# Reading x once in the mixing stage of a two-layer mixture-of-experts kernel: channel-major products, square transposes, permuted rank matrices

## The chip, the core and the metric

The kernel runs on one core of a Trainium2 chip. The metric is device time in microseconds (us), the median of three runs. A profile of one further execution goes with it: its own time, its span (from the first to the last instruction), and every instruction and transfer in it.

Engines, as the profile names them: PE is TensorE (matrix products), PEld its weight loads, DVE is VectorE, ACT is ScalarE, POOL is GpSimd, SP is SyncE, which here only issues transfers. A name with a q at the end (ACTq, SPq) is the engine's queue issuing a transfer.

## The reference, cut to what matters

The input x has 32 batches of 128 rows by 1024 channels, all float32. Two layers follow one another:

```python
# layer 0: each batch picks one of 200 matrices and mixes its rows with it; then a mixture of experts
h = einsum('bct,bcd->bdt', x, weights[cond])        # 32 x 128 tokens x 1024 channels
logits = h @ gate_w.T                               # 64 experts
w, sel = top_k(softmax(logits), 8); w /= w.sum()
# token order fixes the slot of a token at its expert; 256 slots each, later ones are dropped
x = x + scatter_add(w * (silu(inp @ wg) * (inp @ wu)) @ wd)
# layer 1: a linear map with a chosen low-rank part, then a second linear map with 8 gated low-rank parts
x = x + L1_ffn(L1_cond(x))
```

The change concerns the first line and the routing only: how h is made, scored and stored, and how the list of tokens of each expert is found.

## The kernel before, in words

The kernel has three stages. **Stage A** (lines 319 to 552) makes h, routes it and writes it to a buffer in device memory, `hbuf`; on the side it folds weight matrices for the last stage. **Stage B** (lines 658 to 719) is a loop over 64 experts: GpSimd gathers the tokens of an expert from `hbuf`, PE makes the products `pp` and `po`, and GpSimd adds the result to `ybuf`, a second buffer, which has to hold a copy of x by then. **Stage C** (lines 917 to 1021) is a loop over 16 pairs of batches with the products `pr_c`. Nearly every instruction outside the expert loop is recorded at line 206, since the helper `InOrder` issues it; so the tile names are what tells instructions apart. That helper also keeps the instructions of each engine in the order of the program.

Stage A goes in 8 groups of 4 batches. The steps that the change and the prediction touch:

- `loaded_turned(b)` (line 328) loads batch b of `x_t`, a copy of x that the host has turned so that channels lie on partitions: the tile `xTb`, 512 KB, 4 buffers.
- `loaded_batch(b)` (line 332) has GpSimd gather the mixing matrix of the batch, `w`, by row numbers, and SP load batch b of x with rows on partitions: the tile `x`, 512 KB, 6 buffers. So every batch of x is read in two layouts.
- `scored(g)` (line 344): 8 products per batch with a 128x128 block of `xTb` as weights and 64 columns of the gate matrix moving, into `pxg`; VectorE copies it to `xg`.
- `logits(g, xg)` (line 380): one product per batch of `w` with `xg` gives the 64 scores of each token, `plog`; VectorE finds the best 8, ScalarE takes the exponentials.
- `mixed(b)` (line 362): two products per batch, `w` as weights and 512 columns of x moving, into `ph`; ScalarE copies the one half, VectorE the other, to `h` (3 buffers), which ScalarE's queue writes to `hbuf`.
- `counted(g, mask, wt)` (line 410): products with the triangular matrix `tri` and with `ident` give each token's rank at each expert and its weight, turned (`prk`), which ScalarE copies and writes to `ranks` in device memory; a product with `ones` counts tokens per expert (`pcnt`), which VectorE adds up in `upto`.
- `carried(b)` (line 375): SP copies batch b of x to `ybuf`, from device memory to device memory. 24 batches are copied in the loop, the last 8 after it (line 493).
- `combined(n, d)` (line 429): the side work for stage C, 8 products of 388 columns, `pcw`. 9 such steps lie in the loop of groups, 9 after it.

A product of float32 operands is issued as two PE instructions; so 8 products are 16 instructions in the profile.

Behind the groups, `looked_up` (line 214) finds from `upto` in which batch and at which rank each slot of an expert lies; `fetched` (line 235) gathers those rows of `ranks` with GpSimd (`rkg`); `found` (line 253) turns ranks into token numbers on VectorE, and a small product `prow` spreads them over the four quarters of a token's row; `placed` (line 293) makes row numbers out of them, `slot_row`; `gathered` (line 299) fetches the quarters of the tokens from `hbuf`. Two and a half steps of `combined` stand on PE between the last `counted` and the first `prow`.

Of the kernel before, what the change touches and what calls it, by code (L numbers as in the profile page):

```python
# [8 lines left out]
F32 = mybir.dt.float32  # L9
# [42 lines left out]
def kernel(  # L52
# [6 lines left out]
    x_t: bass.AP,  # L59
    gate_w: bass.AP,  # L60

# [20 lines left out]

    hbuf = dram.tile([NT + P, H], F32, name="hbuf")
# [12 lines left out]
    tri = const.tile([P, P], F32, name="tri")  # L96
    nc.gpsimd.affine_select(
        tri, ones, pattern=[[1, P]], compare_op=ALU.is_ge, fill=0.0, base=0, channel_multiplier=-1
    )
# [30 lines left out]
    nc.vector.tensor_scalar(inquad, quad, -float(Q), pcol, ALU.mult, ALU.add)  # L130
    qmask = const.tile([P, NQ], F32, name="qmask")
# [121 lines left out]
    def found(some, lo, hi):  # L253
        u = some["u"] + lo
        n = (hi - lo) * NJ
        flat = some["batch"][:, lo:hi, :].rearrange("p e j -> p (e j)")
        rank = some["rank"][:, lo:hi, :].rearrange("p e j -> p (e j)")
        rk = some["rk"][:, lo * NJ : hi * NJ, :, :]
        hit = fs.tile([P, n, P], F32, name=f"hit_{u}", tag="hit")
        place = fs.tile([P, n], F32, name=f"place_{u}", tag="place")  # L260
        dve.tensor_tensor(
            hit, rk[:, :, 0, :], rank.unsqueeze(2).to_broadcast([P, n, P]), ALU.is_le
        )
        dve.tensor_reduce(place, hit, AX.X, ALU.add)
        dve.tensor_tensor(
            hit,
            iota_t.unsqueeze(1).to_broadcast([P, n, P]),
            place.unsqueeze(2).to_broadcast([P, n, P]),
            ALU.is_equal,
        )  # L270
        dve.tensor_tensor(hit, hit, rk[:, :, 1, :], ALU.mult)
        mine = slice(u * NJ, u * NJ + n)
        dve.tensor_reduce(slot_w[:, mine], hit, AX.X, ALU.add)
        empty = fs.tile([P, n], F32, name=f"empty_{u}", tag="empty")
        dve.tensor_scalar(empty, flat, float(NB), pcol, ALU.is_equal, ALU.mult)
        dve.tensor_tensor(place, place, empty, ALU.add)
        tok = fs.tile([P, n], F32, name=f"tok_{u}", tag="tok")
        dve.scalar_tensor_tensor(tok, flat, float(P), place, ALU.mult, ALU.add)
        byq = fs.tile([P, n, NQ], F32, name=f"byq_{u}", tag="byq")
        dve.tensor_tensor(  # L280
            byq,
            tok.unsqueeze(2).to_broadcast([P, n, NQ]),
            qmask.unsqueeze(1).to_broadcast([P, n, NQ]),
            ALU.mult,
        )
        dve.tensor_copy(slot_tok[:, mine], tok)
        prow = pf.tile([P, 512], F32, name=f"prow_{u}", tag="prow")[:, 0 : n * NQ]
        pe.matmul(
            prow, spread, byq.rearrange("p s q -> p (s q)"), start=True, stop=True
        )  # L290
        some["prow"] = (slice(u * NJ * NQ, (u * NJ + n) * NQ), prow)

    def placed(some):
        rows, prow = some["prow"]
        dve.tensor_scalar(slot_row[:, rows], prow, float(NQ), quad, ALU.mult, ALU.add)
# [23 lines left out]
    with (  # L319
# [6 lines left out]
        xs, xTs, ws = {}, {}, {}  # L326

        def loaded_turned(b):
            xTs[b] = a6.tile([P, HC, P], F32, name=f"xTb_{b}", tag="xTb", bufs=4)
            sync.dma_start(xTs[b].rearrange("p j c -> p (j c)"), x_t[b])  # L330

        def loaded_batch(b):
# [7 lines left out]
            xs[b] = a6.tile([P, H], F32, name=f"x_{b}", tag="x_t")  # L340
            sync.dma_start(xs[b], x[b])


        def scored(g):
            pxg = pa_sm.tile([P, GB, E], F32, name=f"pxg_{g}", tag="sm")
            for t in range(GB):
                xT_b = xTs.pop(g * GB + t)
                for j in range(HC):
                    pe.matmul(
                        pxg[:, t, :],  # L350
                        xT_b[:, j, :],
                        gw_sb[:, j, :],
                        start=(j == 0),
                        stop=(j == HC - 1),
                    )
            xg = a2.tile([P, GB, E], F32, name=f"xg_{g}", tag="xg")
            dve.tensor_copy(xg, pxg)
            for b in range((g + 1) * GB, min((g + 2) * GB, NB)):
                loaded_turned(b)
            return xg  # L360

        def mixed(b):
            rows = slice(b * P, (b + 1) * P)
            h_sb = a2.tile([P, H], F32, name=f"h_{b}", tag="h_sb", bufs=3)
            for n in range(2):
                cols = slice(n * 512, (n + 1) * 512)
                ph = pa_big.tile([P, 512], F32, name=f"ph_{b}_{n}", tag="big")
                pe.matmul(ph, ws[b], xs[b][:, cols], start=True, stop=True)
                if n == 0:
                    act.copy(h_sb[:, cols], ph)  # L370
                else:
                    dve.tensor_copy(h_sb[:, cols], ph)
            act.dma_start(hbuf[rows, :], h_sb)
# [4 lines left out]


        def logits(g, xg):  # L380
            plog = pa_sm.tile([P, GB, E], F32, name=f"plog_{g}", tag="sm")
            for t in range(GB):
                pe.matmul(plog[:, t, :], ws[g * GB + t], xg[:, t, :], start=True, stop=True)
            top = a2.tile([P, GB, K], F32, name=f"top_{g}", tag="top")
            left = a2.tile([P, GB, E], F32, name=f"left_{g}", tag="left")
            for t in range(GB):
                dve.max(top[:, t, :], plog[:, t, :])
                dve.match_replace(left[:, t, :], top[:, t, :], plog[:, t, :], LOW)
            nmax = a2.tile([P, GB], F32, name=f"nmax_{g}", tag="nmax")
            dve.tensor_scalar(nmax, top[:, :, 0], -1.0, None, ALU.mult)  # L390
            ex = a2.tile([P, GB, E], F32, name=f"ex_{g}", tag="ex")
            for t in range(GB):
                act.activation(ex[:, t, :], plog[:, t, :], AF.Exp, bias=nmax[:, t : t + 1])
            mask = a2.tile([P, GB, E], F32, name=f"mask_{g}", tag="mask")
            dve.tensor_scalar(mask, left, LOW, None, ALU.is_equal)
            return ex, mask

        def weights_of(g, ex, mask):
            wt = a2.tile([P, GB, E], F32, name=f"wt_{g}", tag="wt")
            dve.tensor_tensor(wt, ex, mask, ALU.mult)  # L400
# [5 lines left out]
            return wt  # L406
# [3 lines left out]
        def counted(g, mask, wt):  # L410
            rk_sb = a2.tile([E, GB, 2, P], F32, name=f"rk_{g}", tag="rk", bufs=1)
            for i in range(2):
                prk = pa_sm.tile([E, 2, 2, P], F32, name=f"prk_{g}_{i}", tag="sm")
                for t in range(2):
                    pe.matmul(prk[:, t, 0, :], mask[:, 2 * i + t, :], tri, start=True, stop=True)
                    pe.matmul(prk[:, t, 1, :], wt[:, 2 * i + t, :], ident, start=True, stop=True)
                act.copy(rk_sb[:, 2 * i : 2 * i + 2, :, :], prk)
            act.dma_start(ranks[:, g * GB : (g + 1) * GB, :, :], rk_sb)
            pcnt = pa_sm.tile([P, GB, E], F32, name=f"pcnt_{g}", tag="sm")
            pe.matmul(pcnt, ones, mask, start=True, stop=True)  # L420
            for t in range(GB):
# [3 lines left out]
                else:  # L425
                    dve.tensor_tensor(upto[:, :, b], upto[:, :, b - 1], pcnt[:, t, :], ALU.add)

# [14 lines left out]

        gw_sb = a1.tile([P, HC, E], F32, name="gw_sb")
        loaded_turned(0)
        sync.dma_start(gw_sb.rearrange("p j e -> p (j e)"), gate_w)
        for b in range(1, GB):
            loaded_turned(b)
        for b in range(6):
            loaded_batch(b)
# [7 lines left out]
        NG = NB // GB  # L457
        rest = [(0, d) for d in range(HC + 1)]
        xg = scored(0)
        hws = {0: head_block(0)}  # L460
        lefts = left_block("a", 0, "wd")
        for g in range(NG):
            ex, mask = logits(g, xg)
            for t in range(GB):
                b = g * GB + t
                mixed(b)
                if t == 1:
                    wt = weights_of(g, ex, mask)
                if b + 6 < NB:
                    loaded_batch(b + 6)  # L470
                if b >= 8:
                    carried(b - 8)
            if g == NG - 2:
# [6 lines left out]
            for _ in range((0, 1, 1, 1, 1, 1, 2, 2)[g]):  # L480
                for _ in combined(*rest.pop(0)):
                    pass
            if g + 1 < NG:
                xg = scored(g + 1)
                if g == 0:
                    lefts += left_block("a", 1, "wd")
                    lefts += left_block("a", 2, "wu")
                if g == 4:
                    hws[1] = head_block(1)
            counted(g, mask, wt)  # L490
# [606 lines left out]
```

## Time and profile before

| quantity | value |
|---|---|
| time, median of 3 runs (lowest, highest) | 2785.03 us (2782.26, 2787.5) |
| profiled execution, its own time | 2768.09 us |
| its span | 2766.4 us |
| PE busy in the span | 2729.5 us, 99% |
| DVE, ACT, POOL busy | 57%, 15%, 41% |
| bytes moved by transfers | 585.11 MB, mean 212 GB/s |
| last product of the last `counted` of stage A ends | 218.86 us |
| first product of the expert loop | 277.13 us |
| last expert product ends, stage C's own begin | about 2140 us |

Matrix products overlap one another in the record, and a product that waits for its weights counts as busy; so a busy share of 99% does not mean that PE is at its peak. What a product costs is read from the distance between starts in a row of equal ones. The chain of work that ended last names, at each step, what the step waited for; a product in it is on the path that sets the end. The granted clock (PEclk) says at what share of its full rate PE was allowed to run in a stretch.

### The profile page before, as it was taken

What the parts mean: (1) busy time and instruction counts of PE and PEld (TensorE: products, weight loads), DVE (VectorE), ACT (ScalarE), POOL (GpSimd) and SP (SyncE); (2) the same over time, 40 slices, a digit from 0 to 9 for tenths busy, and PEclk for the clock granted to TensorE, in tenths of its full rate; (3) what the DMA queues carried; (4) which work ended last, traced back from release to release, by engine and by line L of the source; (5) the groups of instructions that cost most, each with busy time, mean ns of one, the idle gap of its engine ahead of it and who ended that gap; (6) DMA issues with size and microseconds to landing.
All of it is one profiled execution on the core that took longest, in us unless ns stands there. A gap on an engine that the chain in (4) does not pass through costs nothing.

```text
span 2766.4 us, 23669 instructions
## 1 busy us (share of the span) xinstructions
PE 2729.5 (99%) x8580; PEld 1513.0 (55%) x8580; DVE 1581.5 (57%) x2521; ACT 408.6 (15%) x792; POOL 1123.1 (41%) x846
## 2 busy tenths in 40 slices
PE   8998999999999999999999999999999899999999
PEld 6765555555555555555555555555555555555554
DVE  2334667666676666766657667576563444444442
ACT  1220111111111111111111111111111000000000
POOL 2105365555655646556465564655451100000000
PEclk9999999999999999999999999999999999999999
DMA  9997777777878878777787777777775522222210
GB/s 349 381 376 263 238 255 227 248 262 225 251 241 243 255 225 252 256 234 248 235 249 254 229 247 253 241 244 238 237 248 153 137 74 62 62 61 65 60 43 38
DMA packets 131141, 585.11 MB, mean 212 GB/s; under 512 B 23312, under 2 KB 50000, under 8 KB 105168
## 3 DMA queue, kind: packets, MB, share of 16 engines
q1 hardware_dynamic: 71136, 405.18, 39.6%
q0 software_dynamic: 51200, 155.24, 24.3%
q10 hardware_dynamic: 8688, 23.17, 2.2%
q8 instruction: 68, 1.11, 0.2%
q14 instruction: 49, 0.40, 0.0%
HBM read 476.45 MB, written 123.83 MB: 217 GB/s over the span
## 4 chain that ended last, share of the span: by engine, by line
PE 96%; DMA 2%; DVE 1%; issue 0%; ACT 0%; SPq 0%; POOL 0%; ACTq 0%; DVEq 0%
PE pp L594 42%; PE po L693 23%; PE pr_c L206 17%; PE pcw L206 4%; PE px L206 2%; PE pxg L206 2%; PE ph L206 2%; PE pth L644 2%; DMA xTb<-in_x_t 1%; DMA hbuf<-h 1%; PE prk L206 1%; PE plog L206 0%; DMA rkg<-ranks,row 0%; PE pg L206 0%; PE pt L206 0%
## 5 line engine op out<-in xcount | busy, mean ns | idle before, releaser
L306 POOL DMA_INDIRECT xin<-hbuf,slot_row x512 | 722.6, 1411 | 159.2 <-issue 151.8
L693 PE MATMUL po<-wd,hTb 128*128 128x512 f32 x1536 | 680.3, 592 | 0.6 <-ACT hTb L646 0.6
L704 POOL DMA_INDIRECT ybuf<-o,slot_tok x128 | 205.3, 1604 | 666.1 <-ACT o L702 465.4
L693 PEld LDWEIGHTS po<-wd,hTb 128*128 128x128 f32 x1536 | 286.8, 190 | 323.7 <-issue 306.1
L594 PE MATMUL pp<-wg,xT 128*128 128x384 f32 x1024 | 351.6, 486 | 0.6 <-ACT G_sb L206 0.6
L594 PE MATMUL pp<-t,s 128*128 128x384 f32 x1024 | 341.9, 487 | 0.0
L594 PEld LDWEIGHTS pp<-t,s 128*128 128x128 f32 x1024 | 193.4, 190 | 141.9 <-issue 23.0
L206 DVE TENSOR_TENSOR u<-p,pp 128x384 f32<-128x384 f32 x64 | 35.4, 554 | 386.4 <-PE pp L594 386.4
L594 PEld LDWEIGHTS pp<-wg,xT 128*128 128x128 f32 x1024 | 189.6, 190 | 119.9 <-ACT G_sb L206 1.2
L702 ACT ACTIVATE o<-po,slot_w 128x512 f32<-128x512 f32 x256 | 175.9, 687 | 494.1 <-PE po L693 489.9
L206 POOL DMA_INDIRECT ab<-in_AT,adapter_rows x32 | 36.6, 1144 | 444.2 <-ACT pxw L206 438.9
L206 PE MATMUL pr_c<-BM,X 128*128 128x512 f32 x480 | 213.7, 592 | 0.0
L206 DVE STREAM_TRANSPOSE xT<-xin 128x1024 f32<-128x1024 f32 x128 | 156.1, 1235 | 67.6 <-DMA xin<-hbuf,slot_row 62.4
L594 PE MATMUL pp<-t,xT 128*128 128x384 f32 x512 | 175.6, 486 | 0.0
L594 PE MATMUL pp<-wu,xT 128*128 128x384 f32 x512 | 175.6, 486 | 0.0
L594 PE MATMUL pp<-wu,s 128*128 128x384 f32 x512 | 175.6, 486 | 0.0
L611 ACT ACTIVATE h<-gate 128x384 f32<-128x384 f32 x128 | 67.2, 525 | 699.6 <-DVE gate L206 699.6
L242 POOL DMA_INDIRECT rkg<-ranks,row x128 | 124.8, 975 | 96.7 <-DMA cwbuf<-cw 58.0
L206 PE MATMUL pr_c<-ts,ss 128*128 128x512 f32 x320 | 142.5, 592 | 1.3 <-DVE ss L206 1.3
L206 PEld LDWEIGHTS pr_c<-BM,X 128*128 128x128 f32 x480 | 88.9, 190 | 100.2 <-issue 100.0
L206 DVE TENSOR_TENSOR u<-u,pp 128x384 f32<-128x384 f32 x128 | 70.6, 551 | 125.0 <-PE pp L594 124.9
L594 PEld LDWEIGHTS pp<-wu,xT 128*128 128x128 f32 x512 | 97.3, 190 | 67.8
(158 smaller groups left out, 2920.4 us busy)
## 6 DMA issues: line engine op xcount, KB each, us to landing
wg<-in_wg SPq DMA_DIRECT2D x64, 1536.0 KB, 7.0
wu<-in_wu SPq DMA_DIRECT2D x64, 1536.0 KB, 9.7
wd<-in_wd SPq DMA_DIRECT2D x64, 1536.0 KB, 7.2
xTb<-in_x_t SPq DMA_DIRECT2D x32, 512.0 KB, 7.0
x<-in_x SPq DMA_DIRECT2D x32, 512.0 KB, 9.1
hbuf<-h ACTq DMA_DIRECT2D x32, 512.0 KB, 6.9
ybuf<-in_x SPq DMA_DIRECT2D x32, 512.0 KB, 8.3
xq<-ybuf SPq DMA_DIRECT2D x64, 256.0 KB, 5.1
```

What stands on the lines that cost most here:

```text
L206: return lambda *args, **kw: kept(op(*args, **kw))
L242: nc.gpsimd.indirect_dma_start(out=some["rk"][:, s, :, :].rearrange("p i t -> p (i t)"), out_offset=None, in_=ranks.rearrange("e b i t -> ...
L306: nc.gpsimd.indirect_dma_start(out=xin[:, q, :], out_offset=None, in_=quarters, in_offset=bass.IndirectOffsetOnAxis(ap=slot_row[:, s : s + ...
L594: nc.tensor.matmul(bank, left[k][:, j, :], right[k][:, j, :], start=(j == 0), stop=(j == HH - 1))
L611: nc.scalar.activation(h, gate, AF.Sigmoid)
L644: nc.tensor.transpose(pt[:, i, :], h[:, i * P : (i + 1) * P], ident)
L693: nc.tensor.matmul(po, hT[j][:, i, :], wd_sb[:, i, cols], start=(i == 0), stop=(i == IC - 1),)
L702: nc.scalar.mul(o_sb[:, cols], po, slot_w[:, s : s + 1])
L704: nc.gpsimd.indirect_dma_start(out=ybuf, out_offset=bass.IndirectOffsetOnAxis(ap=slot_tok[:, s : s + 1], axis=0), in_=o_sb, in_offset=None ...
```

## The change

Stage A loads x once, in one layout, in which the host has regrouped the channels of a row by quarter (`x_q`). It runs batch by batch as a pipeline instead of group by group:

- `mixed(b)` now has 128x128 blocks of x as weights and `w` moving, 128 columns: 8 products per batch in the place of 2, and the result `hT` has channels on partitions. ScalarE copies both halves.
- `as_rows(b)`: VectorE transposes `hT` in squares of 32x32 into `hq`, and `stored(b)` writes that to `hbuf`. Whole blocks stay where they are, so a token's four quarters lie in four places, and tokens come in a permuted order.
- `logits(b)`: 8 products per batch with a block of `hT` as weights and 64 columns of the gate matrix moving. The products `pxg` of old, the copy `xg` and the product of `w` with `xg` go.
- `counted(g)`: the matrices `tri` and `ident` are replaced by `upon` and `order`, with rows permuted, so that ranks and weights come out in the true order. `pcnt` now stands ahead of `prk`, and `ranks` is written in two transfers per group in the place of one.
- `found` gets one more small instruction (`quarter`), and the row number is made by adding `qrow`.
- `carried` is called for all 32 batches in the loop; the calls for the last 8 behind the loop are still there.

```diff
-        def scored(g):
-            pxg = pa_sm.tile([P, GB, E], F32, name=f"pxg_{g}", tag="sm")
...
-                    pe.matmul(pxg[:, t, :], xT_b[:, j, :], gw_sb[:, j, :], ...)
-        def mixed(b):
-            h_sb = a2.tile([P, H], F32, name=f"h_{b}", tag="h_sb", bufs=3)
-            for n in range(2):
-                pe.matmul(ph, ws[b], xs[b][:, cols], start=True, stop=True)
-                if n == 0:
-                    act.copy(h_sb[:, cols], ph)
-                else:
-                    dve.tensor_copy(h_sb[:, cols], ph)
-            act.dma_start(hbuf[rows, :], h_sb)
+        def mixed(b):
+            hT = a2.tile([P, HC, P], F32, name=f"hT_{b}", tag="hT", bufs=4)
+            x_b, w_b = xs.pop(b), ws.pop(b)
+            for n in range(2):
+                ph = pa_big.tile([P, HH, P], F32, name=f"ph_{b}_{n}", tag="big")
+                for j in range(HH):
+                    pe.matmul(ph[:, j, :], x_b[:, n * HH + j, :], w_b, start=True, stop=True)
+                act.copy(hT[:, n * HH : (n + 1) * HH, :], ph)
+            hTs[b] = hT
+        def as_rows(b):
+            hqs[b] = a2.tile([P, NQ, HC, Q], F32, name=f"hq_{b}", tag="hq", bufs=3)
+            dve.transpose(
+                hqs[b].rearrange("p b j c -> p j b c"),
+                hTs[b].rearrange("p j (b i) -> p j b i", i=Q),
+            )
+        def logits(b):
...
+            for j in range(HC):
+                pe.matmul(plogs[g][:, t, :], hT[:, j, :], gw_sb[:, j, :], ...)
...
+        for b in range(NB):
+            mixed(b)
+            if b >= 1:
+                as_rows(b - 1)
+                stored(b - 1)
+            if b >= 2:
+                logits(b - 2)
+            if b >= 3:
+                topped(b - 3)
+            g, t = divmod(b - 7, GB)
+            if t == 0 and g >= 0:
+                powers(g)
+                weights_of(g)
+            elif t == 1 and g >= 0:
+                counted(g)
+            if b + 6 < NB:
+                loaded_batch(b + 6)
...
+            for _ in range(2 if b in (12, 16, 20, 24) else int(b >= 4)):
+                carried(next(copies))
+            if b in (8, 11, 14, 17, 20, 23, 26):
+                some_rows()
...
         part = {0: looked_up([0, 1, 2, 3])}
         fetched(part[0], 4 * NJ)
         for b in range(NB - 8, NB):
             carried(b)
```

`topped(b)` holds the search for the best 8 of one batch, `powers(g)` the exponentials, `some_rows()` one step of `combined(0, d)`. The nine steps `combined(1, d)` behind the loop and everything after them are unchanged. The pool of `plog`, `prk` and `pcnt` has three banks before and after.

## The prediction

> **What bounds the kernel now.** I read the chain of waits first. From 277.13 us to the end it is PE almost without a break, and the change does nothing there; so whatever stage A gains or loses moves the end by as much. The stage has one clear mark: the last `counted` ends at 218.86. In the chain, a group of four batches at full pace looks like this (start, length, what):
>
> ```profile
> 84.51 7.09 PE pxg L206 x64
> 91.60 1.89 PE prk L206 x16
> 93.49 0.63 PE pcnt L206 x2
> 94.12 0.84 PE plog L206 x8
> 94.96 6.92 PE ph L206 x16
> 101.88 5.21 PE pcw L206 x16
> ```
>
> Without `pcw` that is 17.37 us a group. Eight groups and nine `pcw` steps make 139.0 + 46.9 = 185.9 us of PE work. The stage takes 218.9, so 33.0 are lost. The chain tells where: elsewhere it runs over transfers instead of products, and after them PE is slow.
>
> ```profile
> 6.53 13.90 PE pxg L206 x64
> ...
> 22.90 8.61 PE ph L206 x16
> ...
> 45.76 7.68 DMA hbuf<-h
> ...
> 53.50 6.90 DMA xTb<-in_x_t
> ...
> 60.44 7.09 PE pxg L206 x32
> 67.52 3.38 PE prk L206 x16
> ```
>
> The first 64 `pxg` take 13.90 where others take 7.09; after the wait for `xTb`, 32 take what 64 should. The table by stretches (start:end, length, busy us of PE, PEld, DVE, ACT, POOL, then granted clock, transfer share, GB/s) agrees:
>
> ```profile
> 40.00:60.00 20.00, 18.06 (x79) 11.24 (x77) 7.17 (x26) 4.46 (x11) 3.78 (x4) 1.00 1.02 413
> 60.00:80.00 20.00, 19.56 (x77) 15.01 (x78) 6.80 (x26) 3.74 (x9) 3.40 (x4) 0.74 1.02 417
> ...
> 180.00:200.00 20.00, 17.93 (x98) 16.12 (x97) 2.07 (x9) 2.12 (x4) 0.00 (x0) 0.74 0.95 358
> ```
>
> Transfers fill the engines (a share of 1.0 at 413 and 417 GB/s), PE idles a little, and then the granted clock falls to half for some 10 us. The loss splits into 6.5 us before the first product; 9.6 of slow start (13.90, 8.61 and a `plog` of 1.97 against 7.09, 6.92, 0.84); two slow spells, 5.0 (at 60.44: 3.5 for `pxg`, 1.5 for `prk`) and 4.7 (at 187.4); and the rest, about 7, of idling. So stage A is bound by PE and transfers together, neither far from its limit.
>
> **Transfers.** The rows of the table up to 220 us add to 81.0 MB. The change takes out 32 loads of 0.524 MB (16.8 MB) and puts in 8 more copies to `ybuf` (4.2 MB), since the last 8 calls of `carried` are now in the loop and still stand after it; x is thus read 72 batches' worth in place of 96, where one reading is 32. Left are 68.4 MB: at 410 GB/s 167 us. That falls below PE's work, so transfers should stop setting the pace, by a margin of some 10 per cent only.
>
> **Products.** Removed per batch: 8 products `pxg` (16 instructions) and one `plog`; added: 8 `plog` products of the same shape as `pxg`. That is a change of -0.84 us a group, -6.7 in all. `ph` goes from 4 instructions of 512 columns (6.92/16 = 433 ns) to 16 of 128 columns with a weight load each. No row shows 128 columns on 128x128 weights, but two lie on either side (the second from the timeline of PE, stage C):
>
> ```profile
> 2213.47 4.30 PE L206 MATMUL px<-pxw,X 128*128 128x152 f32 x32
> 2217.61 4.45 PE L206 MATMUL pr_c<-ts,ss 128*128 128x512 f32 x10
> ```
>
> 64 columns run at 7.09/64 = 111 ns an instruction, so the weight load sets that pace and hides the product; 152 columns run at (2217.61-2213.47)/32 = 129 ns, so the product sets it (512 columns take 433, 0.85 ns each) and hides the load. For 128 columns both are about 109; I take 111, with 109 and 129 as nearest bounds, and as the far one the two in series, 111 + 108 = 219. That makes 512 x 0.111 = 56.8 us for all of `ph`, against 8 x 6.92 = 55.4: +1.4. The sum of PE's work: 56.8 + 56.7 (`plog`) + 8 x 2.52 (`counted`) + 46.9 = 180.6.
>
> *A rule against the change.* The Trainium skill, "TensorE: Matmul & The Clock Gate", section "Back-to-back issue gap", gives for streams of load and product about 81 ns at 128 columns and 131 at 512, so that four narrow products cost 2.5 times a wide one. Scaled to the 433 ns above, the new `ph` would take 268 ns an instruction and 80 us more in all, and the change would lose. The rows at 64 and 152 columns speak against it here, and I go by them.
>
> **Start.** The first product now needs `w`, not `xTb`. Its gather is issued at 4.99 us and the first two take 5.4 to land: 10.5 against 6.53, so +4.0. The gate matrix, waited for before, is needed later.
>
> **The slow clock.** In three slow spells the rate came back 2.4 to 5.3 us after products of 128 columns and more had begun (22.90 to 26.2; 194.4 to 196.8; 239.4 to 244.7), while `pxg` ran on at half rate for 16 and 7 us. Now the first products are of 128 columns: 2.5 us lost at the start, not 9.6 (that is the upper bound). The two later spells go with the waits that led to them.
>
> *On this,* the same page, section "Part 1: The HAM clock gate", frees the clock after one busy window of about 3.4 us. The trace disagrees for the first spell, which lasted 19.7 us of nearly unbroken work, under a granted clock that reads 1.00. By the rule the start would lose 1.7.
>
> **New waits.** With three banks, `prk`'s second half takes the bank of `pcnt`, which VectorE must first read. Behind it on PE wait `pcw` or the next `ph`. In the trace `pcnt` starts at 218.16 and `upto` ends at 220.08, 1.9 us later; PE gets there after 0.53 + 0.87 = 1.4, so 0.5 us eight times, and up to 1.2 more each when a transpose stands ahead of `upto`: 4 to 14, I take 5. The steps of ScalarE and VectorE lie two or three batches behind the product they serve and are covered:
>
> ```profile
> L206 DVE STREAM_TRANSPOSE xT<-xin 128x1024 f32<-128x1024 f32 x128 | 156.1, 1235 | 67.6 <-DMA xin<-hbuf,slot_row 62.4
> ```
>
> VectorE gains 4 transposes of 1.235 a group and loses 4 copies of 0.688 and one of 0.425: +1.8 on 6 to 7 us of work per 20. ScalarE gains 4 copies of 0.59: about 7 per 20. If that cover failed, the four `hT` buffers would stop PE. ScalarE's queue also issues 8 more `ranks` transfers (0.45 each), behind which its copies wait; SP issues 24 fewer. Early on, before `pcw` begins, a batch asks 1.7 MB in 4.2 us, all that transfers give, and three weight blocks besides; six loaded batches cover most of it. I put 2 us for that. GpSimd's gathers of `w` keep their number and lie six batches ahead.
>
> **Behind the mark** 13 us of `pcw` wait on PE while ranks are fetched; PE then idles:
>
> ```profile
> 222.92 0.45 ACTq L206 DMA_DIRECT2D ranks<-rk  x1
> ...
> 226.91 0.95 POOL L242 DMA_INDIRECT rkg<-ranks,row  x1 [58.00 <-DMA cwbuf<-cw]
> ...
> 238.94 0.59 PE L206 MATMUL prow<-byq,spread 128*128 128x8 f32 x2 [7.04 <-DVE byq L206]
> ```
>
> `prk` now ends last, 0.6 later against the mark than before: +0.6. The issue at 222.92 came 4 us after the copy it sends was done, waiting for a queue that `ybuf` copies filled; if that goes, -4; if two transfers wait instead of one, +4. I take 0. The extra `quarter` (0.16 us) and the expert loop's VectorE work cost nothing: PE covers them.
>
> **Sum.** 10.5 + 180.6 + 2.5 + 5 + 2 + 0.6 = 201.2 against 218.9: **-17.7 us**. The profiled execution took 2768.09 (span 2766.40, 1.7 outside it), so 2750.4. The median of the runs lies 16.9 above that; I let the same offset stand: 2785.0 - 17.7 = **2767**.
>
> **Rivals.**
> - *Transfers still end last* (20 in 100). Before, the stage lost 33 us with 167/198 of the present load. If the waits for `hbuf` writes and their slow spells stay half as large (about 8 us more than I put), the mark comes at 209 to 214 and the time is 2775 to 2780. For it: only 10 per cent of margin, and transfers in flight are few. Against: stores now come evenly, not four in 7 us.
> - *The weight load is not hidden at 128 columns* (8 in 100). Then 512 x 0.108 = 55 us more: 2822, slower. It decides from a pace of 111 + 17.7/0.512 = 146 ns upward. Against it stand 111 and 129.
> - *The clock stays at half through the stage's alternation of 64 and 128 columns* (4 in 100): half a us lost per us, no gain from 35 us on.
> - *Better than forecast* (10 in 100): no bank waits and the rank path 4 us shorter, 2756 to 2759.
> - Forecast as it stands: 58 in 100, 2759 to 2775.
>
> **Numbers.** The range runs from the better case, 2756, to the end of the first rival, 2780. About 0.2% (5.6 us) is what a measurement can tell from no change, so faster means below 2779.5: 58 + 10 + most of the first rival, 0.82. Same: the rest of it and half the clock's, 0.08. Slower: 0.10.
>
> **What would show it.** Right: `ph` in runs of 16 at about 111 ns, no `DMA hbuf` or `xTb` in the chain before the mark, granted clock 1.00 after the first 20 us, the mark near 201 and the first expert product near 259, 572.5 MB moved. Wrong: `ph` instructions at 146 ns or more; a stretch at 0.74; PE idle behind ScalarE's copies; a first product later than 12 us.

## The result and the profile after

The changed kernel takes 2751.83 us (median of 4 runs, 2750.44 to 2753.03) against 2783.65 for the kernel before (4 runs, 2781.56 to 2787.50): 31.8 us less, a ratio of 0.9884 [0.9862, 0.9907]. The direction was forecast, the size was not: 17.7 us were forecast, and the time lies 4 us below the range. The profiled execution of the changed kernel has a span of 2749.5 us and a time of 2751.29, almost what the prediction gave for it (2750.4). That nearness was luck, as the experiments show.

In stage A the prediction holds. The chain of waits of the changed kernel (start, length, what), here the start and the first `counted`:

```profile
5.00 5.57 DMA w<-in_cond_w,cond_rows
10.61 8.40 PE ph L212 x48
19.01 1.73 PE plog L212 x16
20.75 1.84 PE ph L212 x16
...
43.62 0.27 DVE upto L212
44.03 1.06 PE prk L212 x8
45.09 5.41 PE pcw L212 x16
50.50 1.78 PE ph L212 x16
```

Each step has 16 instructions: `ph` takes 1.84/16 = 115 ns an instruction, `plog` 1.73/16 = 108. Where the chain leaves PE, it goes over VectorE's `upto` to `prk`, the wait for a bank that was foreseen; no transfer stands in it between 11 us and the mark. The same stretches as before, in the table of the changed kernel (busy us of PE, PEld, DVE, ACT, POOL, then granted clock, transfer share, GB/s):

```profile
40.00:60.00 20.00, 19.66 (x143) 16.77 (x141) 8.10 (x21) 5.83 (x11) 3.12 (x4) 1.00 1.02 418
60.00:80.00 20.00, 19.66 (x142) 16.77 (x141) 8.88 (x26) 6.14 (x14) 3.48 (x4) 1.00 1.02 419
...
180.00:200.00 20.00, 18.92 (x100) 13.42 (x99) 8.54 (x32) 4.33 (x13) 0.00 (x0) 1.00 0.48 171
```

Transfers are still full (1.02) early on, but PE works 19.66 of 20 us and the clock stays at 1.00; and near the end of the stage transfers are at 0.48, where they were at 0.95 before. The last `prk` ends at 200.5, the mark; 201.2 was forecast. Behind the mark the timeline of the changed kernel (start, length, engine, line, what, idle time before it and what ended it) looks other than forecast:

```profile
213.79 0.39 PE L212 MATMUL prow<-byq,spread 128*128 128x8 f32 x2
...
219.33 0.28 PE L212 MATMUL prow<-byq,spread 128*128 128x8 f32 x2
...
227.83 0.23 DVE L212 TENSOR_SCALAR slot_row<-prow,qrow 128x8 int32<-128x8 f32 x1 [10.08 <-remote]
...
230.72 0.48 ACT L212 COPY cw<-pcw 128x388 f32<-128x388 f32 x1 [12.30 <-remote]
...
232.46 0.61 PE L212 MATMUL prow<-byq,spread 128*128 128x16 f32 x2 [7.53 <-DVE byq L212]
```

PE's wait of 7.04 us at the first `prow` is gone. In its place PE waits 7.53 at the third, because VectorE stood still until 227.83 and ScalarE until 230.72, though the products that they needed had been done since 219.6 and 222. The releaser is "remote": a signal came at that moment, but no work that the profile shows had ended just before it. So the first expert product came at 259.13, where it was forecast, but by another way.

### The profile page after: what moved, and what is told of

It is laid out like the page before. It is cut to its first block, busy times and chain, and to the rows that moved or that the text cites. A ratio compares the mean times of both kernels' runs of the same rounds, so it can differ in the third digit from the quotient of the medians.

```text
span 2749.5 us, 24289 instructions
## 1 busy us (share of the span) xinstructions
PE 2709.0 (99%) x8900; PEld 1522.9 (55%) x8900; DVE 1597.9 (58%) x2535; ACT 426.6 (16%) x824; POOL 1118.7 (41%) x845
## 2 busy tenths in 40 slices
DMA packets 127430, 572.55 MB, mean 208 GB/s; under 512 B 23056, under 2 KB 49744, under 8 KB 101328
## 3 DMA queue, kind: packets, MB, share of 16 engines
q0 software_dynamic: 51200, 155.24, 24.4%
## 4 chain that ended last, share of the span: by engine, by line
PE 96%; DVE 2%; issue 1%; DMA 1%; another core or an unknown queue 0%; ACT 0%; ACTq 0%; SPq 0%; DVEq 0%
PE pp L633 41%; PE po L732 24%; PE pr_c L212 17%; PE pcw L212 4%; PE px L212 2%; PE ph L212 2%; PE plog L212 2%; PE pth L683 2%; DMA wu<-in_wu 0%; DVE upto L212 0%; DVE hit L212 0%; PE pg L212 0%; PE prk L212 0%; PE pt L212 0%
## 5 line engine op out<-in xcount | busy, mean ns | idle before, releaser
L633 PEld LDWEIGHTS pp<-t,xT 128*128 128x128 f32 x512 | 97.2, 190 | 68.3 <-DVE u L212 0.7
```

The lines of the kernel that those rows point to most:

```text
L633: nc.tensor.matmul(bank, left[k][:, j, :], right[k][:, j, :], start=(j == 0), stop=(j == HH - 1))
```

## The experiments

One table first, from the profiles of the runs told of below. The mark is the end of the last product of the last `counted`; the hand-over is the time from there to the first expert product; the rest is the span behind that. "Landing" says whether the profile gives a time from issue to landing for transfers; what that means is told under a7 to b7.

| kernel | landing | mark | PE's wait at a prow | hand-over | first expert product | rest |
|---|---|---|---|---|---|---|
| before, first profile | yes | 218.9 | 7.0 (first) | 58.3 | 277.1 | 2489.3 |
| b1, before | yes | 217.7 | 8.1 (first) | 58.9 | 276.6 | 2491.4 |
| b2, before | yes | 215.1 | 13.9 (first) | 64.2 | 279.3 | 2491.1 |
| b4, before | no | 216.5 | 14.1 (first) | 75.6 | 292.2 | 2492.0 |
| b7, before | no | 212.2 | 13.6 (first) | 73.8 | 286.0 | 2491.8 |
| b5, before, warm products | no | 217.8 | 7.9 (first) | 68.4 | 286.2 | 2493.7 |
| b3, 4 batches of turned x loaded | yes | 207.8 | none | 47.7 | 255.5 | 2490.3 |
| b6, last copies later | yes | 221.3 | none | 48.2 | 269.4 | 2494.4 |
| after, first profile | no | 200.5 | 7.5 (third) | 58.6 | 259.1 | 2490.4 |
| a2, after | no | 203.4 | 5.5 (third) | 69.3 | 272.7 | 2490.0 |
| a7, after | no | 204.0 | 8.8 (third) | 59.2 | 263.1 | 2490.3 |
| a3, after, 24 copies in the loop | no | 207.4 | 8.3 (third) | 58.3 | 265.7 | 2490.1 |
| a1, after, 16.8 MB more | yes | 229.8 | 7.1 (first) | 57.4 | 287.3 | 2490.1 |
| a4, after | yes | 202.7 | none | 47.9 | 250.6 | 2491.1 |
| a5, after, block moved | yes | 205.5 | 0.2 (first) | 48.1 | 253.6 | 2492.2 |
| a8, after, fewer gathers | no | 207.0 | 1.1 (second) | 49.5 | 256.5 | 2491.4 |
| a6, after, improved | yes | 194.6 | 1.0 (first) | 48.8 | 243.4 | 2491.3 |
| a9, after, improved | no | 194.7 | 1.3 (first) | 59.6 | 254.3 | 2489.7 |

The rest is 2489 to 2494 us in every one. So a kernel's time is settled, but for these 5 us, when its first expert product starts, and the differences lie in the mark and in the hand-over. In every run whose span is known, the time is the span and about 1.7 us.

### b1, b2, b4: is the offset fixed?

The kernel before, unchanged, on two chips.

> The kernel before, unchanged, with a new profile. The profiled execution of before (2768.09 us) was 13.5 to 19.4 us shorter than its timed ones, and the kernel after shows no such offset. Theory A: the offset lies in stage A; ordinary executions of before lose more to transfers and to the half clock than the one profiled. Then a profile of an execution of about 2783 us has the end of the last counted at 232 to 235 us instead of 218.9, more or longer waits on DMA in the chain before it, and the same 2489 us from the first expert product to the end. Theory B: the offset lies behind stage A or outside the span. Then the mark stays near 219 and the excess shows later, or the span is 15 us shorter than the time.

> The kernel before once more, a second profile: theory A expects the mark and the time to move together, us for us, over the profiles of before; theory B expects a mark near 219 whatever the time.

> The kernel before once more, beside the kernel after on the same chip. In the last call its 23 timed executions lay at 2764 to 2776 us, where those of the forecast's own measurement lay at 2782 to 2788. Theory A (how late transfers are differs from chip to chip and run to run, and before is exposed to it): on another chip the median differs again by several us, with waits on DMA in stage A and behind its mark as the part that differs. Theory B (a fixed offset between the profiled and the timed execution): time and profile differ by the same 15 us wherever it is run.

Measured: b1 2771.42 (2767.33 to 2775.47, 10 runs), b2 a single run of 2772.12, b4 2776.90 (2768.22 to 2790.65, 10 runs). The offset of 16.9 us is no constant of the measurement: each time is its span and about 1.7 us. The first profile of before was simply of a shorter execution than its timed runs. b4's profile is of a run as long as those (2785.86), and its mark is at 216.5, earlier than the 218.9 of the first profile. The excess lies behind the mark, in the timeline of b4:

```profile
243.67 0.60 PE L206 MATMUL prow<-byq,spread 128*128 128x8 f32 x2 [14.12 <-DVE byq L206]
...
290.70 0.48 ACT L206 COPY cw<-pcw 128x388 f32<-128x388 f32 x1 [10.90 <-remote]
...
292.15 5.16 PE L594 MATMUL pp<-wg,xT 128*128 128x384 f32 x8 [10.16 <-ACT G_sb L206]
```

PE waits twice as long for the ranks as in the first profile, and 10.16 us more because ScalarE stood still without a releaser, as in the changed kernel. b4's hand-over is 17.4 us longer than that of the first profile, and the two spans differ by 17.8.

### b3 and a1: the bytes or the order of the work?

b3 is the kernel before with only the first 4 batches of the turned x loaded, so routing is of other tokens, and 14.7 MB less are read:

```diff
-            xTs[b] = a6.tile([P, HC, P], F32, name=f"xTb_{b}", tag="xTb", bufs=4)
+            xTs[b] = a6.tile([P, HC, P], F32, name=f"xTb_{b}", tag=f"xTb{b}", bufs=1)
...
-                xT_b = xTs.pop(g * GB + t)
+                xT_b = xTs[t]
...
-            for b in range((g + 1) * GB, min((g + 2) * GB, NB)):
-                loaded_turned(b)
```

> The kernel before with only the first four turned batches loaded; every group is scored on them, so 28 loads (14.7 MB) and their waits go and the routing is that of other tokens, all other work stays. Theory A (transfers, not PE work, made the excess): the slow spells and waits go, the mark comes at 6.5 + 186 + 9.6 of slow start and some 2 of waits, about 204, so 2750 to 2757 us. Theory B: the profiled loss of about 17 goes and the offset stays, 2765 to 2772. If the waits were on stores in bursts and not on the bytes, less than 10 us go.

a1 is the changed kernel with 16.8 MB put back as copies that nobody reads, one in each `loaded_batch`:

```diff
             sync.dma_start(xs[b].rearrange("p j c -> p (j c)"), x_q[b])
+            sync.dma_start(dead[b * P : (b + 1) * P, :], x[b])
 
         def carried(b):
```

> The kernel after with 32 further copies of 0.524 MB each from x to an unused buffer in device memory, one behind each load of x: the bytes of stage A go back to 85 MB, the form of the work stays. Theory A: transfers end last again, the waits and slow spells come back: 10 to 35 us more, 2762 to 2787 us. Rival: the even spacing of loads and stores, not the bytes, is what helps; then less than 5 us more, under 2757.

Measured, on one chip with the kernel before at 2770.20: b3 2745.88, a ratio of 0.9914 [0.9898, 0.9931]; a1 2781.64, 1.0046 [1.0029, 1.0063]. Taking bytes out of the old order of work gives 24 us. Putting them into the new order costs the whole gain and more: on another chip with landings the changed kernel takes 2742.48 (a4 below), so 16.8 MB cost some 39 us; the kernel before differs by 2 us between these two chips. In b3, against b1, the mark comes 10 us sooner and the hand-over is shorter by another 11. The table by stretches of a1 shows what full transfers do to the new order:

```profile
40.00:60.00 20.00, 15.45 (x83) 11.35 (x83) 4.40 (x11) 3.51 (x7) 1.89 (x2) 0.83 1.03 421
180.00:200.00 20.00, 12.58 (x79) 11.36 (x79) 6.69 (x17) 4.81 (x11) 0.00 (x0) 0.74 1.02 380
```

PE works 12.58 to 15.45 of 20 us, and with the idle time the half clock comes back (0.74 to 0.83). So the gain goes with the bytes; with them put back, the new order of work is not faster than the old. The swap is not exact: a1 moves about 85 MB up to the mark, where before moves 81, and its extra copies go from device memory to device memory and stand on SP's queue right behind each load of x.

### b5: what was the slow start?

The kernel before with 16 products of 128 columns of the identity ahead of `scored`:

```diff
+        warm = pa_sm.tile([P, P], F32, name="warm", tag="sm")
+        for _ in range(16):
+            pe.matmul(warm, ident, ident, start=True, stop=True)
```

> The kernel before with 16 products of 128 columns (identity by identity, result unused) on PE ahead of the first pxg, while it waits for its data. If products of 128 columns bring the full rate within some 3 us and those of 64 do not, the first 64 pxg take about 7 us and not 13.9: up to 9 us less to the second group, of which transfers may take back a part (5 to 9 us off the time). If the slow start depends on time since the start and not on the shape, nothing is gained, or up to 2 us lost.

Measured: 2772.24 (10 runs), a ratio of 0.9972 [0.9952, 0.9991] to a kernel before of 2782.74. The chain of b5:

```profile
1.54 5.77 PE warm L206 x32
7.30 7.19 PE pxg L206 x64
...
27.87 14.50 DMA x<-in_x
...
42.42 11.73 DMA xTb<-in_x_t
```

The first 64 `pxg` take 7.19 us and not 13.90: products of 128 columns bring the full rate within 5.8 us, products of 64 did not in 13.9. The granted clock says the same, if it is read from the trace's own list of grants: the first entry, full clock, stands at 26.16 us in before, 3.3 after the first `ph`, and at 5.61 in b5. The 1.00 that the table by stretches prints for the time ahead of the first entry is no reading. What PE wins is given back: the next waits for `x` and `xTb` are 14.50 and 11.73 us, and the mark is at 217.8. The gain of 0.28% is hardly more than what the unchanged b4 shows beside it (0.15%). In the kernel before, the slow start lay beside transfers that had to be waited for anyway.

### a2 and a3: the changed kernel on the chip of b4, and its repeated copies

a2 is the changed kernel; a3 copies 24 batches in the loop and the last 8 behind it, so that none is copied twice:

```diff
-            for _ in range(2 if b in (12, 16, 20, 24) else int(b >= 4)):
+            if b >= 8:
```

> The kernel after on the same chip. Theory A: 2750 to 2753 us as in its first measurement, on any chip, since its chain holds few waits on transfers; so the ratio to before goes with before: 0.988 where before is 2783, 0.993 where it is 2770. Theory B: after moves with before by the same amount, and the difference stays near 17 or near 32 us everywhere.

> The kernel after with each batch of x copied to ybuf once: 24 copies in the loop, 8 behind it, 4.2 MB less. If the margin of transfers is thin, the waits left (half a us each at prk aside) go, 1 to 3 us less; if transfers no longer set the pace, the same time within 2 us.

Measured: a2 2754.53 (2753.28 to 2764.45), 0.9896 [0.9864, 0.9927]; a3 2757.59 (2755.59 to 2768.02), 0.9915 [0.9885, 0.9946]. So 4.2 MB less gave nothing. a2's profile is of its longest execution, with another such standstill, of 13 us, in which PE started single `pcw` products 2.1 to 3.5 us apart:

```profile
242.82 0.49 PE L212 MATMUL pcw<-hw,WB_a 128*128 128x388 f32 x1 [0.75 <-issue]
246.31 0.81 PE L212 MATMUL pcw<-hw,WB_a 128*128 128x388 f32 x1 [3.00 <-issue]
248.41 0.81 PE L212 MATMUL pcw<-hw,WB_a 128*128 128x388 f32 x1 [1.30 <-issue]
```

### b6: are the ranks late because of the last copies?

The kernel before; the last 8 copies to `ybuf` leave SP's queue ahead of the ranks and go out on ScalarE's queue, late in the hand-over:

```diff
-        for b in range(NB - 8, NB):
-            carried(b)
...
             next(step)
+            if d >= 5:
+                for b in range(NB - 18 + 2 * d, NB - 16 + 2 * d):
+                    act.dma_start(ybuf[b * P : (b + 1) * P, :], x[b])
```

> The kernel before with one thing moved: the last 8 copies of x into ybuf (4.2 MB) are no longer put on SP's queue just ahead of the gathers of ranks, but go out on ScalarE's queue, two after each of the last four steps of combined(1, d). The four profiles of the kernel before so far have the mark at 215 to 218.9 us and the first expert product at 276.4, 277.1, 279.1 and 292.2; behind that product all four need 2490 to 2492 us. So what differs from execution to execution lies between the mark and the first expert product. Theory A (the copies hold up the ranks: VectorE's wait for rkg is 12.8 to 19.8 us there and 7.8 in the changed kernel): that wait falls to 10 or less, PE's wait at the first prow from 7 to 14 us to 3 or less, the first expert product comes at 268 to 273, the median is 5 to 12 us below that of the kernel before on the same chip, and the spread of its runs, 12 us on one chip and 24 on another, halves. Theory B (the spread comes from stalls of PE that no transfer in the records ends, like the 10 us at 282 to 292 us of one profile and the 13 us at 241 to 254 of one of the changed kernel): the ranks may come sooner, but the spread stays at 12 to 24 us. Theory C: the ranks are late because of the ranks' own writes and gathers, and nothing moves: within 3 us.

Measured: 2767.05 (2762.44 to 2773.30, 10 runs) against 2772.11 (13 runs, 2765.65 to 2780.33), 0.9984 [0.9970, 0.9998]. The timeline of b6:

```profile
234.12 0.28 PE L206 MATMUL prow<-byq,spread 128*128 128x8 f32 x2
239.55 0.28 PE L206 MATMUL prow<-byq,spread 128*128 128x8 f32 x2
244.99 0.29 PE L206 MATMUL prow<-byq,spread 128*128 128x16 f32 x2
269.41 2.85 PE L595 MATMUL pp<-wg,xT 128*128 128x384 f32 x8 [0.57 <-ACT G_sb L206]
```

PE no longer waits at the first `prow`; VectorE's wait for `rkg` is 5.5 us where before had 12.8 to 19.8, and the hand-over is 48.2 us, 10 less than in the shortest profile of before. Theory A holds for the ranks. Only half of it reaches the time, 5 us by medians: in this profile the mark is 2 to 6 us later than in the three profiles of before with landings, and the rest 3 to 5 longer; the copies now lie beside the loads of the first experts' weights, but that they cost those 3 to 5 us is not shown. The spread of the runs, 10.9 us against 14.7, did not halve. In the four profiles of the changed kernel VectorE's wait for `rkg` is 7.7 to 7.8 us, though its last 8 copies still stand ahead of the ranks: its transfers have room by then (0.48 in 180 to 200 us). In a1, where they are full to the mark, it is 14.9.

### a4, a5, a6: variants of the changed kernel

a5 moves one block; a6 does that and four more things:

```diff
-            elif d == 4:
+            elif d == 6:
                 found(part[0], 2, 4)
```

```diff
-            pcnt = pa_sm.tile([P, GB, E], F32, name=f"pcnt_{g}", tag="sm")
+            pcnt = pf.tile([P, 512], F32, name=f"pcnt_{g}", tag="prow")[:, 0 : GB * E]
...
+        for _ in range(16):
+            pe.matmul(warm, ident, ident, start=True, stop=True)
...
-            if b == 25:
+            if b == 28:
...
-        for b in range(NB - 8, NB):
-            carried(b)
```

> The changed kernel again, as the yardstick for the two variants of it beside it: median 2751 to 2755 us, mark 200 to 204 us, PE waits 7 to 8 us at the third prow, first expert product near 259. Whether the kernel before on this chip lies at 2770 or at 2783 says whether the gain is 17 or 30 us; if the spread of the kernel before is that of its hand-over, the changed kernel's own median stays within 4 us of 2752 on any chip.

> The changed kernel with one block moved: found(part[0], 2, 4), looked_up and fetched for the next four experts stand at step 6 of combined(1, d) in the place of step 4, so that two more steps of PE's work (6.6 us) lie ahead of the third prow. Theory A (the idle time of PE at the third prow, 7.5 us, is on the path that sets the end, since VectorE is busy with the row numbers of the first two experts and the ranks of the others are long there): PE idles 1 us or less there, the first expert product comes 6 to 8 us sooner, near 252, and the median is 6 to 8 us below the changed kernel's. Rival: the first expert product waits for its tokens or its weights instead (in the changed kernel the tokens' last transpose and sum end 249 to 250 us): it comes at 256 to 259 and the gain is 0 to 3 us.

> The changed kernel with five small things, all read from its profile: the block of found(part[0], 2, 4) at step 6; the counts pcnt in a bank of their own (that of prow), so that prk's second half no longer waits for VectorE; 16 products of 128 columns of the identity matrix ahead of the first ph, while PE waits for w; the zero rows stored after batch 28 in the place of batch 25; the 8 repeated copies of x behind the loop left out (they write what is already there). If the losses add up: bank waits 3.4 us, slow start 3, third prow 7.5, so the mark comes at 194 to 196 us, the first expert product at 246 to 249, and the median lies 10 to 14 us below the changed kernel's, at 2738 to 2742. If what PE wins is given back to the transfers, as in the kernel before with warm products, the mark stays at 198 or later and only the 7 us of the third prow are won, or less.

Measured on one chip (before 2772.11): a4, the changed kernel, 2742.48 (2739.59 to 2744.62), 0.9888 [0.9861, 0.9914]; a5 2744.79 (2743.33 to 2747.62); a6 2737.70 (2736.50 to 2739.04), 0.9874 [0.9849, 0.9899]. The changed kernel is 10 us below its first time, and a5 gains nothing. The timeline of a4 tells why:

```profile
221.84 0.23 DVE L212 TENSOR_SCALAR slot_row<-prow,qrow 128x8 int32<-128x8 f32 x1 [2.17 <-PE prow L212]
...
226.95 0.29 PE L212 MATMUL prow<-byq,spread 128*128 128x16 f32 x2
```

VectorE does not stand still, so PE does not wait at the third `prow`, and there is nothing for a5 to win. That wait is no property of the changed kernel. a6's mark is 8.1 us earlier than a4's (194.6), as expected; its median is 4.8 us below, where 10 to 14 were expected, 7.5 of them from that wait. It is the shortest kernel of the study: 34 us below the kernel before on that chip.

### a7, a8, a9, b7: do the standstills go with the chip and with GpSimd's gathers?

The profiles with a standstill had something else in common. In the list of transfers of the changed kernel's first profile, and of a4 (operation, count, KB each, median us from issue to landing):

```profile
wg<-in_wg SPq DMA_DIRECT2D x64, 1536.0 KB
rkg<-ranks,row POOLq DMA_INDIRECT x128
```

```profile
wg<-in_wg SPq DMA_DIRECT2D x64, 1536.0 KB, 7.2
rkg<-ranks,row POOLq DMA_INDIRECT x128, 5.8
```

Where landings are missing, they are missing for every transfer of every queue, since signals that tell of them are not in the trace: between the first gather of ranks and the first expert product the first profile of the changed kernel holds 96 signals for 38 gathers, a4 464 for 31. What the trace has of the signals that PE sends also differs. In a4, as in every profile with landings, a signal of PE in the hand-over comes 0.01 us after the product that sends it. In the first profile of the changed kernel, products that send one ended at 219.49, 219.61 and 222.32, and signals came at 224.98, 227.80 and 230.70; VectorE went on at 227.83 and ScalarE at 230.72. So "remote" stands here for a signal that came late, not for late work. a8 takes GpSimd's gathers for the first two experts out of the hand-over; these experts work on zeros:

```diff
             xin = fs.tile([P, NQ, W4], F32, name=f"xin_{e}_{j}", tag="xin", bufs=4)
-            for q in range(NQ):
+            if e < 2:
+                pool.memset(xin, 0.0)
+            for q in range(NQ if e >= 2 else 0):
```

> The changed kernel once more, as the yardstick. Two kinds of profile have come back so far. In the one kind (before, b1, b2, b3, b6, a1, a4, a5, a6) the gathers on GpSimd's queue show a landing; in the other (b4, b5, after, a2, a3) they show none, and only there do PE, VectorE and ScalarE stand still for 8 to 14 us behind the mark with no releaser but issue or remote. All runs of one chip are of one kind. If that is so, this run is either of the first kind, with 2740 to 2745 us and the kernel before at 2769 to 2773 beside it, or of the second, with 2750 to 2756 and the kernel before at 2777 to 2784.

> The changed kernel without the gathers of the first two experts' tokens: GpSimd fills those four tiles with zeros, so the 32 indirect transfers that stand on its queue between the first and the last prow are 16 fewer, and the first two experts work on zeros. Theory A (the stalls behind the mark, in the kind of execution that has them, go with GpSimd's row of gathers): on a chip of that kind this kernel has no such stall in the stretch of the first three prow, PE idles under 2 us at the third, and it is 6 to 10 us faster than the changed kernel beside it; on the other kind of chip it is within 3 us of it, since PE does not wait there. Rival (the stalls are of the chip's signals at large, whatever GpSimd issues): on a chip of that kind they stay, and the gain is under 3 us.

> The version with the five small things, on another chip. On a chip of the first kind again 2736 to 2740 us and 4 to 6 us below the changed kernel; on one of the second kind its moved block covers the wait at the third prow too, so it should be 8 to 14 us below the changed kernel there, at 2739 to 2746.

> One look at the kernel before on this chip. If the kinds go with the chip, its profile is of the same kind as the others of this call: with landings, the mark at 215 to 219, PE's wait at the first prow 7 to 14 us, the first expert product at 276 to 280 and a time of 2766 to 2775; without landings, the first expert product at 285 to 293 and 2777 to 2786.

Measured, on a chip where all four profiles lack the landings (before 2782.17, 8 runs, 2769.63 to 2790.80): a7, the changed kernel, 2762.86 (2755.19 to 2763.38), 0.9933 [0.9900, 0.9966]; a8 2745.42 (2745.08 to 2749.68); a9, the kernel of a6, 2749.68 (2742.65 to 2755.31); b7 2779.47. The timeline of a7, then of a8:

```profile
232.49 0.23 DVE L212 TENSOR_SCALAR slot_row<-prow,qrow 128x8 int32<-128x8 f32 x1 [11.53 <-remote]
232.58 0.48 ACT L212 COPY cw<-pcw 128x388 f32<-128x388 f32 x1 [10.16 <-remote]
...
237.11 0.61 PE L212 MATMUL prow<-byq,spread 128*128 128x16 f32 x2 [8.75 <-DVE byq L212]
```

```profile
227.74 0.23 DVE L212 TENSOR_SCALAR slot_row<-prow,qrow 128x8 int32<-128x8 f32 x1 [0.40 <-PE prow L212]
230.45 0.48 ACT L212 COPY cw<-pcw 128x388 f32<-128x388 f32 x1 [5.47 <-PE pcw L212]
232.85 0.29 PE L212 MATMUL prow<-byq,spread 128*128 128x16 f32 x2
```

Without that row of gathers neither VectorE nor ScalarE stands still, PE's signals, as far as they are recorded, come at most 0.85 us late, and the median falls by 17.4 us, more than the 6 to 10 that were expected; the hand-over, 49.5 us, is about a4's, which has its gathers. Theory A holds: on such a chip the standstills go with GpSimd's gathers. That a8 gains nothing on a chip with landings was not run. Over four chips (8 and 3 with landings, 10 and 2 without; four profiles on each) the kind went with the chip, whatever the kernel; each chip was used on one occasion only, so chip and occasion cannot be told apart. a7 is slower than its expectation by 7 us, and a9 is above its own by 4: a9 has no wait at the third `prow`, but the standstill struck `pcw` instead (single products 1.4 to 2.1 us apart, from 226 to 236 us). b7 came as expected for its kind, with its first expert product at 286.0. Why the gathers delay signals of engines that do not wait for them is not shown by any record here. One rival is open: every execution here, the timed ones too, carries a recorded span and clock, so it is not known whether such chips stand still when nothing is recorded.

## Why the prediction was right or wrong

**Stage A: right, nearly term by term.** Start 10.5, measured 10.61. `ph` at 111 ns, measured 115, which is 2 us more in all; the narrow products cost about what the rows at 64 and 152 columns said. Slow start 2.5, measured 8.40 - 3 x 1.84 = 2.9; the trace's first entry of full clock is at 16.47 us, 5.9 after the first `ph`. One reading on the way was wrong: the 1.00 for the clock of the first spell, since the trace has no entry ahead of 26.16. Bank waits 5, measured 3.4 (7 waits of PE for `upto`, at most 1.3). Early transfers 2, measured about none. Mark 201.2, measured 200.5, and 202.7 to 204.0 in a2, a4 and a7. Bytes 572.5 MB, measured 572.55. The mark of before was less sure than its one profile said: five profiles have it at 212.2 to 218.9, the first one latest. From the mean of these five, 216.1, to that of the four of the changed kernel, 202.7, stage A gains 13.4 us, where the two first profiles give 18.4.

**The rival that transfers still end last: fell.** Their share is 1.02 from 20 to 120 us, yet PE waits for none. a1 shows that the margin is smaller than 16.8 MB: with that much more, PE waits for x and the mark comes at 229.8. How much smaller was not measured.

**"Behind the mark ... I take 0": wrong.** This term was bounded at -4 and +4. Between profiles with landings it measured -10.3: the hand-over went from 58.3 us (first profile of before) to 47.9 (a4); from b1 and b2 it is -11.0 and -16.2. PE's 7.0 us at the first `prow` went, 2.8 of half clock after it (8.33 us from first to second `prow`, 5.54 in a4), and 0.6 at the first expert product. The sum for that pair is -16.2 at the mark, -10.3 in the hand-over, +1.8 in the rest: -24.7, from a span of 2766.4 to 2741.7. The prediction named the cause, an issue that waited for a queue full of `ybuf` copies, and priced only the 4 us of that issue. Behind it the transfers themselves were late: b6 and b3 show that without those copies, or without that backlog, PE does not wait at all at the first `prow`. Thinner transfers in stage A were counted until the mark; they go on paying behind it.

**"I let the same offset stand": wrong, and this step put the number out of its range.** The changed kernel's profile took 0.9 us more than the 2750.4 that were forecast for it, but its median lies 0.5 above that profile, not 16.9. The 16.9 us had been taken as a constant. They are time in the hand-over, in the ranks' wait and the standstills: 58 and 59 us in the two shortest profiles of before, 64 to 76 in the three longer ones. Most likely the first profile of before and its three timed runs come from chips of the two kinds; on chips with landings its median is 2770 and 2772 and no run is longer than 2780.3, on the others it is 2782 and 2783. That is not shown, since those three runs left no profile.

**Why the profiled time came out right all the same.** By luck: the forecast left out two things that cancelled. The hand-over got 10 us shorter, and the changed kernel's first profile, without landings, has a standstill that put 10 back. Compared within one chip, the medians fell by 28.2 and 29.6 us (a2, a4; 22.4 for a2 against b4's ten runs) and by 19.3 (a7, whose own runs spread over 8 us); the first measurement gave 31.8. In the pair b7 and a7, both without landings, the spans differ by 24.4: 8.2 at the mark, 14.6 in the hand-over, 1.5 in the rest (with rounding).

**The rules that were weighed.** By an estimate scaled from the Trainium skill's "Back-to-back issue gap" (page "TensorE: Matmul & The Clock Gate") `ph` would have cost 268 ns an instruction; measured 115. The rows of the trace were the better guide.

## What to carry to other kernels

When a change thins out transfers, follow the backlog past the stage that it belongs to: what is queued at the stage's end delays the first small, urgent transfer of the next, and its price is the wait at the far end, not the late issue. Before a forecast is added to a median, find out in which stretch the profiled execution and the timed ones differ; if the change touches that stretch, the offset is part of the forecast. A wait that stands in one profile alone should be seen in a second, on another chip, before it is moved or removed: a5 moved one that was not there. And a figure that a view prints where the trace has no record, as the clock of 1.00 ahead of the first entry, is not a measurement.

## What the runs showed of the hardware

- On two of four chips, signals are missing from the traces, and in the hand-over signals of PE come late while GpSimd issues a row of gathers, most of them 1.25 us apart: VectorE stands still for 8.0 to 11.5 us (a2, after, a3, a7), and PE waits 10.2 and 10.6 ahead of the first expert product (b4, b7). Taking 16 gathers out removed that (a8, 17.4 us by medians). On the two other chips the same program has no standstill, and the signals come within 0.01 us. In the longest standstills PE starts single products 1.4, 2.1 or 3.5 us apart (a2, a9), all multiples of 0.7, and the profile names nothing that it waits for.
- Sustained float32 products of 64 columns did not bring PE to its full clock in 13.9 us (before, first entry of full clock at 26.16 us); products of 128 columns did within 5.8 us in b5 and 5.9 in the changed kernel (entries at 5.61 and 16.47). Later spells of half clock last 3.41, 6.83, 10.24, 13.65 or 17.07 us in these traces, all multiples of 3.41.
- float32 products on 128x128 weights cost 108 ns an instruction at 64 columns and 115 at 128: up to there, narrowing a product gains next to nothing, and widening one from 64 to 128 costs 7 ns.
